# Twelve linear-attention layers and a feed-forward block: TensorE's steps of the middle layers in a written order

## The chip, the cores and the metric

The kernel runs on one core of a Trainium2 chip. The metric is the time of one execution on the device, in microseconds (us); lower is better. The engines are called PE (TensorE; PEld is its weight loads), DVE (VectorE), ACT (ScalarE), POOL (GpSimd) and SP (SyncE, which here only issues transfers).

## The reference

The input is 16 sequences of 256 tokens with 128 features. It passes 12 attention layers without softmax, a layer norm over input plus result, a feed-forward block with 384 hidden features and integer weights, and a second layer norm.

```python
for i in range(12):                      # 16 heads of 8 features
    q, k, v = split(x @ Wqkv[i].T + bqkv[i])
    att = einsum('bhqd,bhkd->bhqk', q, k) / sqrt(8)
    x = einsum('bhqk,bhkd->bhqd', att, v) @ Wproj[i].T + bproj[i] + x
x = layernorm(x0 + x)
h = silu(x @ (w_gate/127).T) * (x @ (w_up/127).T)
x = layernorm(x + h @ (w_down/127).T)
```

## The kernel before

Without a softmax a layer is linear in its tokens, so the kernel never carries the 256 tokens through the layers. For each sequence it carries a state of 128 x 130 numbers (`tst`): what the layers so far have made of a token's 128 features, and a column for the offsets (biases and means). The Gram matrix G of the centred tokens (`g0`) is computed once, in the prologue. One layer is then, for each pair of sequences (`thl` is the state as a rounded part hi and a residual lo, `whl` the weights in the same way):

1. k and v (`kv`): six matmuls of 256 columns of the state with the weights (lines 439 to 441), three for each sequence: hi with the rounded weights, hi with their residual, lo with the rounded weights. A copy brings them from the bank to `kv`.
2. G v (line 460): two full-precision matmuls of 128 columns, which the profile shows as four rows; a copy to `gv`.
3. q (lines 447 to 449): three matmuls of 260 columns; a copy, and a small DVE operation for the offsets (line 453).
4. M = k' G v, head group by head group (line 504): small matmuls of 32 x 32 tiles for all four pairs of a set at once. With it run the offset products (line 385), which multiply the offset column of a set's states with the weights. DVE makes of them `vb`, `kb`, a transpose and their product `kvo` (lines 395 to 400 and 212), adds `kvo` to M (line 514, `gm`) and multiplies with a mask (line 212).
5. y (line 522): 32 small matmuls, `gm` with q.
6. The projection (lines 539 to 541): y is copied to a rounded part and a residual (`yhl`, lines 204, 206 and 535), three matmuls follow for each pair, and DVE adds the result to the state (line 546). ACT rounds the state to hi (line 204, `thl`), POOL subtracts to lo (line 209). With these the next layer begins.

The 16 sequences form eight pairs, and these two sets of four; the sets run half a layer apart, so that PE works on one while the other engines work on the other. A half-layer on PE holds one run of M, one of y, 24 matmuls for k and v, 12 for q, 12 projections and 8 for G v.

The order of the instructions isn't written by hand. The program text declares operations with costs, the values that they read and write, the engines that can do them and a due time (`prio`); `Plan.run` goes through a model of the engines' time, always takes a ready operation that can start first (among equals the one with the earliest due time), gives it an engine and a PSUM bank (eight of them), and emits it. Each engine then works through its own list in that order; semaphores make it wait where a value isn't there yet. Copies from banks can go to ACT or DVE, subtractions to lo to POOL alone.

The due times are in the main loop: set `o` of layer `l` is due at `l + 0.5 * o`, q 0.3 later (`QLATE`), and the offsets' DVE work 0.3 later (`OFFSET`). From layer 2 on (`OWN`) the offset products of one set ride in the M run of the other: `heads(l, o, ...)` gets the rider `(l + o, 1 - o)`. In steady state the planner's order for PE is: offsets and M; one pair's q; k and v of two pairs of the other set; y; k and v of the other two; one G v; the projections; three G v; three pairs' q; and the same again for the other set.

Beside the layers, each layer's weights are loaded, rounded to `whl` (by DVE mostly, line 206), their residual subtracted (POOL, line 209), and turned copies of the projection weights made by transfers (`wpt`). In the last two layers and after them comes the feed-forward block for the eight pairs (`ffn`), with its norms on DVE (`st`), POOL and ACT.

Of the kernel before, what the change touches and what calls it, by code (L numbers as in the profile page):

```python
# [14 lines left out]
ALU = mybir.AluOpType  # L15
# [3 lines left out]
L = 12  # L19
# [21 lines left out]


OSTEP = 0.5
OFFSET = 0.3
LATE = 0.02
OWN = 2
DEEP = 0.5
QLATE = 0.3
FOFF = -1
FSTEP = 0.15  # L50
LSTEP = 0.05
# [41 lines left out]
class Plan:  # L93
# [23 lines left out]
    def run(self):  # L117
# [8 lines left out]
        while ready:  # L126
            found = []
            for o in ready:
                if any(not slots[v.kind] for v in takes(o)):
                    continue  # L130
                held = max((min(slots[v.kind])[0] for v in takes(o)), default=0.0)
                best, least = None, None
                for e, c in o.costs.items():
                    t = max(free[e], held)
                    for d in o.deps:
                        wait = TO_PE if e == PE and d.engine in (ACT, DVE, POOL) else 30 if d.engine == e == PE else AFTER[d.engine]
                        t = max(t, d.end + wait)
# [32 lines left out]
def mmr(n):  # L170
    return max(111, 0.447 * n + 5)
# [19 lines left out]
def linear_attention_ffn_kernel(ctx: ExitStack, tc: tile.TileContext, x, xt, wall, wq0, bias, wg, wu, wd, out):  # L191
# [228 lines left out]
    gms = [new(f"gm{o}", [OB, 32]) for o in range(NO)]  # L420
    vgm = sets()

    def products(l, p, prio):

        raw, whv, _ = wts[l]
        bs = slice(p * PB, (p + 1) * PB)
        hl = lambda i, s, n=1: whl[whv.slot][:, i, s * C : (s + n) * C]
        hi, lo = thl[p][:, 0], thl[p][:, 1]
        kv, qs, gv = kvs[p], qss[p], gvs[p]
        if l == 0:  # L430
            tv = lambda b: wraw[raw.slot][:, 2 * C : 3 * C]
            src = raw
        else:
            pkv, pq = Val("bank"), Val("bank")

            def mm_kv(e):
                for b in range(PB):
                    o = bank(pkv)[:, b * 2 * C : (b + 1) * 2 * C]
                    nc.tensor.matmul(o, hi[:, b, 0:C], hl(0, 1, 2), start=True, stop=False)  # L439
                    nc.tensor.matmul(o, hi[:, b, 0:C], hl(1, 1, 2), start=False, stop=False)  # L440
                    nc.tensor.matmul(o, lo[:, b, 0:C], hl(0, 1, 2), start=False, stop=True)  # L441
            plan.op({PE: 6 * mmr(256)}, mm_kv, [vhi[p], vlo[p], whv], [pkv], prio)
            plan.op({ACT: act(512), DVE: dve(512)}, lambda e: copy(e, kv.rearrange("p a b c -> p (a b c)"), bank(pkv)), [pkv], [vkv[p]], prio)

            def mm_q(e):
                o = bank(pq)[:, : PB * W]
                nc.tensor.matmul(o, hl(0, 0), flat(hi), start=True, stop=False)  # L447
                nc.tensor.matmul(o, hl(0, 0), flat(lo), start=False, stop=False)  # L448
                nc.tensor.matmul(o, hl(1, 0), flat(hi), start=False, stop=True)  # L449
            plan.op({PE: 3 * mmr(PB * W)}, mm_q, [vhi[p], vlo[p], whv], [pq], prio + QLATE)  # L450
            q = lambda: bank(pq)[:, : PB * W].rearrange("p (b w) -> p b w", w=W)
            plan.op({ACT: act(PB * C), DVE: dve(PB * C)}, lambda e: copy(e, qs[:, :, 0:C], q()[:, :, 0:C]), [pq], [vq[p]], prio + QLATE)
            plan.op({DVE: 130}, lambda e: nc.vector.tensor_scalar(qs[:, :, C], q()[:, :, C], bcol[:, l, 0:1], None, ALU.add), [pq, vbias], [vqo[p]], prio + QLATE)  # L453
            tv = lambda b: kv[:, b, 1, :]
            src = vkv[p]
        pgv = Val("bank")

        def mm_gv(e):
            for b in range(PB):
                nc.tensor.matmul(bank(pgv)[:, b * C : (b + 1) * C], g0[p][:, b, :], tv(b), start=True, stop=True)  # L460
        plan.op({PE: 2 * mm32()}, mm_gv, [vg0[p], src], [pgv], prio)
        plan.op({ACT: act(256), DVE: dve(256)}, lambda e: copy(e, flat(gv), bank(pgv)[:, : PB * C]), [pgv], [vgv[p]], prio)
        if l == L - 1:

            def rest(e):
                copy(e, tst[:, bs, 0:C], center.unsqueeze(1).to_broadcast([128, PB, C]))
                copy(e, tst[:, bs, C], mb[:, bs])
            plan.op({ACT: act(PB * C, True) + 100, DVE: dve(PB * C, True) + 75}, rest, [vhi[p], vlo[p], vmb], [vt[p], vc[p]], prio)

    def first_q(o, prio):  # L470

# [11 lines left out]
    def heads(l, o, prio, riders):  # L483

        raw = wts[l][0]
        pairs = range(o * G, (o + 1) * G)
        gm = gms[o]
        pm, pys = Val("bank"), [Val("bank") for _ in pairs]  # L490
        group = lambda g: slice(32 * (g % G), 32 * (g % G) + 32)
        src = [raw] if l == 0 else [vkv[p] for p in pairs]

        more = [(*r, *offset_products(*r)) for r in riders]

        def mm_m(e):
            for _, _, _, _, mm in more:
                mm()
            for p in pairs:
                for b in range(PB):  # L500
                    n = (p - o * G) * PB + b
                    tk = wraw[raw.slot][:, C : 2 * C] if l == 0 else kvs[p][:, b, 0, :]
                    for g in range(G):
                        nc.tensor.matmul(bank(pm)[group(g), n * 32 : n * 32 + 32], tk[:, group(g)], gvs[p][:, b, group(g)], start=True, stop=True)  # L504
        reads = [v for _, _, rs, _, _ in more for v in rs]
        if l == 0 and o == 1:

            reads += vw[:G]
        plan.op({PE: 890 + 140 * len(more)}, mm_m, [*(vgv[p] for p in pairs), *src, *reads], [pm, *(m[3] for m in more)], prio)
        for lo, oo, _, pc, _ in more:  # L510
            offsets(lo, oo, prio + (OFFSET if lo else 0), pc)
            if lo == 0:
                first_offsets(o, prio)
        plan.op({DVE: dve(OB * 32)}, lambda e: nc.vector.tensor_tensor(
            gm, bank(pm)[:, : OB * 32].rearrange("p (b j) -> p b j", j=32), kvo[:, o * OB : (o + 1) * OB], ALU.add), [pm, vkvo[o]], [vgm[o]], prio)
        plan.op({DVE: dve(OB * 32), POOL: pool(OB * 32)}, lambda e: mul(e, gm, gm, mask32.unsqueeze(1).to_broadcast([128, OB, 32])), [], [vgm[o]], prio)

        def mm_y(e):
            for b in range(PB):
                for r, p in enumerate(pairs):  # L520
                    for g in range(G):
                        nc.tensor.matmul(bank(pys[r])[group(g + r), b * W : (b + 1) * W], gm[group(g), r * PB + b, :], qss[p][group(g), b, :], start=True, stop=True)  # L522
        plan.op({PE: 1200}, mm_y, [vgm[o], *(vq[p] for p in pairs), *(vqo[p] for p in pairs)], pys, prio)
        return pys

    def projection(l, p, py, prio):
# [10 lines left out]
        def mm_w(e):  # L537
# [7 lines left out]
        plan.op({PE: (3 if l < L - 1 else 5) * mmr(PB * W)}, mm_w, [vyh[p], vyl[p], vhi[p], vlo[p], whv, turned], [pw, vw[p]], prio)  # L545
        plan.op({DVE: dve(PB * W)}, lambda e: nc.vector.tensor_tensor(ts, bank(pw)[:, : PB * W], ts, ALU.add), [pw], [vt[p], vc[p]], prio)  # L546
        if l < L - 1:
            plan.op({ACT: act(PB * W, True)}, lambda e: copy(e, flat(hi), ts), [vt[p], vc[p]], [vhi[p]], prio)
# [168 lines left out]
    for l in range(L):  # L717
        if l + 1 < L:
            prep_weights(l + 1)
        for o in range(NO):  # L720
            at = l + OSTEP * o
            for p in range(o * G, (o + 1) * G):
                products(l, p, at)
            for r, py in enumerate(heads(l, o, at, [(l, o)] * (l < OWN) + [(l + o, 1 - o)] * (OWN <= l + o < L))):
                projection(l, o * G + r, py, at + (LSTEP * r if l == L - 1 else 0))
        if l < NP:
            center_tokens(l, l + 2)
    prep_ffn(L - 2)
# [34 lines left out]
```

## Time and profile before

| | us |
|---|---|
| median of three runs | 309.67 (308.54 to 309.88) |
| the profiled execution | 309.26 |
| its span | 307.20 |
| PE busy (share of the span) | 297.3 (97%) |
| DVE busy | 227.2 (74%) |
| ACT busy | 221.3 (72%) |
| POOL busy | 136.4 (44%) |

The profile is of one execution. Its span runs from the first to the last instruction that it shows; about 2 us lie outside. Busy times are those in which an engine had an instruction in it; matmuls overlap in PE, so a full-width matmul of 256 columns shows a length of 0.28 us but the next one starts 0.12 us later, and starts are what to compare. The mean clock that the throttle granted PE over the span is 0.989 of full speed.

### The profile page before, as it was taken

What the parts mean: (1) busy time and instruction counts of PE and PEld (TensorE: products, weight loads), DVE (VectorE), ACT (ScalarE), POOL (GpSimd) and SP (SyncE); (2) the same over time, 40 slices, a digit from 0 to 9 for tenths busy, and PEclk for the clock granted to TensorE, in tenths of its full rate; (3) what the DMA queues carried; (4) which work ended last, traced back from release to release, by engine and by line L of the source; (5) the groups of instructions that cost most, each with busy time, mean ns of one, the idle gap of its engine ahead of it and who ended that gap; (6) DMA issues with size and microseconds to landing.
All of it is one profiled execution on the core that took longest, in us unless ns stands there. A gap on an engine that the chain in (4) does not pass through costs nothing.

```text
span 307.2 us, 12904 instructions
## 1 busy us (share of the span) xinstructions
PE 297.3 (97%) x5384; PEld 272.3 (89%) x5384; DVE 227.2 (74%) x680; ACT 221.3 (72%) x571; POOL 136.4 (44%) x234
## 2 busy tenths in 40 slices
PE   8999999999999999999999999999999999999971
PEld 8989999999999999999999999999999988888840
DVE  3797887777677676776767877787554699899993
ACT  2547877867768677777677666776986768968964
POOL 6246353334541345314453144521442456568582
PEclk9999999999999999999999999999999999999995
DMA  7534213122031120311202112130000000000214
GB/s 211 149 99 128 71 39 89 35 55 71 9 82 38 42 84 2 90 37 43 82 4 53 38 28 55 30 81 2 4 2 3 2 1 2 0 0 22 83 34 137
DMA packets 22489, 15.65 MB, mean 51 GB/s; under 512 B 1952, under 2 KB 19872, under 8 KB 22432
## 3 DMA queue, kind: packets, MB, share of 16 engines
q1 hardware_dynamic: 21872, 14.62, 17.5%
q8 instruction: 42, 0.69, 0.9%
q10 hardware_dynamic: 560, 0.22, 0.3%
q14 instruction: 15, 0.12, 0.1%
HBM read 8.02 MB, written 2.10 MB: 33 GB/s over the span
## 4 chain that ended last, share of the span: by engine, by line
PE 88%; DVE 7%; ACT 3%; issue 1%; POOLq 0%; POOL 0%
PE bank L460 14%; PE bank L439 8%; PE bank L522 8%; PE bank L441 7%; PE bank L440 7%; PE bank L447 5%; PE bank L504 5%; PE bank L541 4%; PE bank L539 4%; PE bank L540 4%; PE bank L448 3%; PE bank L449 3%; PE bank L341 3%; PE bank L665 2%; PE bank L681 2%; PE bank L682 2%
## 5 line engine op out<-in xcount | busy, mean ns | idle before, releaser
L209 POOL TENSOR_TENSOR thl<-tst,thl 128x260 fp32r<-128x260 f32 x88 | 64.5, 764 | 122.9 <-ACT thl L204 122.9
L204 ACT COPY qgv<-bank 128x256 f32<-128x256 f32 x171 | 60.8, 376 | 20.5 <-PE bank L449 13.5
L204 ACT COPY kv<-bank 128x512 f32<-128x512 f32 (+1 forms) x93 | 53.3, 575 | 18.6 <-PE bank L441 13.4
L439 PE MATMUL bank<-whl,thl 128*128 128x256 f32 x176 | 51.8, 294 | 0.0
L441 PE MATMUL bank<-whl,thl 128*128 128x256 f32 x176 | 49.6, 282 | 0.0
L440 PE MATMUL bank<-whl,thl 128*128 128x256 f32 x176 | 49.4, 281 | 0.0
L460 PE MATMUL bank<-kv,g 128*128 128x128 f32 x352 | 46.0, 275 | 0.0
L546 DVE TENSOR_TENSOR tst<-bank,tst 128x260 f32<-128x260 f32 x96 | 36.9, 425 | 11.9 <-PE bank L541 9.1
L204 ACT CAST thl<-tst 128x260 fp32r<-128x260 f32 x88 | 33.0, 408 | 14.6 <-DVE tst L546 14.5
L460 PEld LDWEIGHTS bank<-kv,g 128*128 128x128 f32 x352 | 42.7, 191 | 0.4 <-issue 0.4
L453 DVE TENSOR_SCALAR qgv<-bank,bcol 128x2 f32<-128x2 f32 x88 | 19.3, 221 | 27.6 <-ACT qgv L204 23.0
L439 PEld LDWEIGHTS bank<-whl,thl 128*128 128x128 f32 x176 | 33.1, 188 | 4.1 <-issue 4.0
L535 DVE TENSOR_TENSOR yhl<-bank,yhl 128x260 fp32r<-128x260 f32 x96 | 34.3, 421 | 2.4 <-ACT yhl L204 2.4
L440 PEld LDWEIGHTS bank<-whl,thl 128*128 128x128 f32 x176 | 33.2, 189 | 0.0
L441 PEld LDWEIGHTS bank<-whl,thl 128*128 128x128 f32 x176 | 33.1, 188 | 0.0
L447 PE MATMUL bank<-thl,whl 128*128 128x260 f32 x88 | 29.0, 329 | 0.0
L522 PE MATMUL bank<-qgv,gm 32*32 32x130 f32 x1536 | 25.9, 280 | 0.2 <-DVE gm L212 0.2
L204 ACT CAST yhl<-bank 128x260 fp32r<-128x260 f32 (+1 forms) x61 | 22.3, 418 | 5.2 <-PE bank L522 3.8
L206 DVE CAST yhl<-bank 128x260 fp32r<-128x260 f32 x43 | 16.5, 424 | 11.8 <-PE bank L522 11.8
L448 PE MATMUL bank<-thl,whl 128*128 128x260 f32 x88 | 24.8, 282 | 0.0
L449 PE MATMUL bank<-thl,whl 128*128 128x260 f32 x88 | 24.7, 281 | 0.0
L522 PEld LDWEIGHTS bank<-qgv,gm 32*32 32x32 f32 x1536 | 17.3, 103 | 5.6 <-ACT kv L204 0.3
(153 smaller groups left out, 705.8 us busy)
## 6 DMA issues: line engine op xcount, KB each, us to landing
wraw<-wall SPq DMA_DIRECT2D x12, 256.0 KB, 3.0
wpt<-whl SPq DMA_DIRECT2D x24, 96.0 KB, 2.2
qgv<-x SPq DMA_DIRECT2D x8, 256.0 KB, 5.4
xt<-xt SPq DMA_DIRECT2D x8, 256.0 KB, 3.3
out<-kv SPq DMA_DIRECT2D x7, 256.0 KB, 2.3
wpt<-whl SPq DMA_DIRECT2D x24, 64.0 KB, 2.6
wpt<-whl SPq DMA_DIRECT2D x24, 32.0 KB, 1.9
wraw<-wg SPq DMA_DIRECT2D x1, 192.0 KB, 3.4
```

The lines of the kernel that those rows point to most:

```text
L204: nc.scalar.copy(dst, src)
L209: (nc.vector if e == DVE else nc.gpsimd).tensor_tensor(dst, a, b, ALU.subtract)
L439: nc.tensor.matmul(o, hi[:, b, 0:C], hl(0, 1, 2), start=True, stop=False)
L440: nc.tensor.matmul(o, hi[:, b, 0:C], hl(1, 1, 2), start=False, stop=False)
L441: nc.tensor.matmul(o, lo[:, b, 0:C], hl(0, 1, 2), start=False, stop=True)
L447: nc.tensor.matmul(o, hl(0, 0), flat(hi), start=True, stop=False)
L448: nc.tensor.matmul(o, hl(0, 0), flat(lo), start=False, stop=False)
L449: nc.tensor.matmul(o, hl(1, 0), flat(hi), start=False, stop=True)
L460: nc.tensor.matmul(bank(pgv)[:, b * C : (b + 1) * C], g0[p][:, b, :], tv(b), start=True, stop=True)
L522: nc.tensor.matmul(bank(pys[r])[group(g + r), b * W : (b + 1) * W], gm[group(g), r * PB + b, :], qss[p][group(g), b, :], start=True, stop= ...
L535: plan.op({DVE: dve(PB * W)}, lambda e: nc.vector.tensor_tensor(yl, bank(py)[:, : PB * W], yh.bitcast(F32), ALU.subtract), [py, vyh[p]], [ ...
L546: plan.op({DVE: dve(PB * W)}, lambda e: nc.vector.tensor_tensor(ts, bank(pw)[:, : PB * W], ts, ALU.add), [pw], [vt[p], vc[p]], prio)
```

## The change

The one function that declared q, k, v and G v of a pair (`products`) is cut into `keys_values`, `queries` and `gram_values`; the M step (`heads`) and the y step (`outputs`) become two functions as well. In the layers from 1 to 10 each of PE's operations also writes a value `order` that stands for nothing but the order: as each must wait for the one declared before it, PE's list there is exactly that of the main loop. A run of M for set `o` of layer `l` is followed by k and v of the other set's next step (layer `l + o`, set `1 - o`), its G v, then y of set `o`, q of the other set, and the projections of set `o`. The matmuls for k and v are declared in two parts, two with hi alone and then the other four, but in the middle layers they stand side by side. The offset products of a set now run in the set's own M run, in all layers. The due times for q and for the offsets' DVE work lose their delay, and in the planner's model a PE operation that needs another PE operation no longer waits 30 ns for it. All engines but PE, and PE in layer 0 and in layer 11 with the feed-forward block, are still planned as before.

In the order of the built program the other engines differ as follows: 13 copies of G v move from DVE to ACT, and ten of the adds of the projection bias to the offset column (`share`, lines 405 and 407) from POOL to ACT. The number of matmuls of each kind is the same.

The main loop and the pieces that set the order:

```diff
-OFFSET = 0.3
-OWN = 2
-QLATE = 0.3
...
-                        wait = TO_PE if e == PE and d.engine in (ACT, DVE, POOL) else 30 if d.engine == e == PE else AFTER[d.engine]
+                        wait = TO_PE if e == PE and d.engine in (ACT, DVE, POOL) else 0 if d.engine == e == PE else AFTER[d.engine]
...
+    order = Val()
+    line = lambda l: [order] if 0 < l < L - 1 else []
+
+    def keys_values(l, p, prio):
...
+        def mm_hi(e, b=0):
+            o = bank(pkv)[:, b * 2 * C : (b + 1) * 2 * C]
+            nc.tensor.matmul(o, hi[:, b, 0:C], hl(0), start=True, stop=False)
+            nc.tensor.matmul(o, hi[:, b, 0:C], hl(1), start=False, stop=False)
+        plan.op({PE: 2 * mmr(256)}, mm_hi, [vhi[p], whv], [pkv, *line(l)], prio)
+
+        def mm_lo(e):
+            for b in range(PB):
+                if b:
+                    mm_hi(e, b)
+                nc.tensor.matmul(bank(pkv)[:, b * 2 * C : (b + 1) * 2 * C], lo[:, b, 0:C], hl(0), start=False, stop=True)
+        plan.op({PE: 4 * mmr(256)}, mm_lo, [vlo[p], whv], [pkv, *line(l)], prio)
...
-        plan.op({PE: 3 * mmr(PB * W)}, mm_q, [vhi[p], vlo[p], whv], [pq], prio + QLATE)
+        plan.op({PE: 3 * mmr(PB * W)}, mm_q, [vhi[p], vlo[p], whv], [pq, *line(l)], prio)
...
-        plan.op({PE: 2 * mm32()}, mm_gv, [vg0[p], src], [pgv], prio)
+        plan.op({PE: 2 * mm32()}, mm_gv, [vg0[p], *src], [pgv, *line(l)], prio)
...
-        more = [(*r, *offset_products(*r)) for r in riders]
+        offs, pc, mm_c = offset_products(l, o)
 
         def mm_m(e):
-            for _, _, _, _, mm in more:
-                mm()
+            mm_c()
             for p in pairs:
...
-        plan.op({PE: 890 + 140 * len(more)}, mm_m, [*(vgv[p] for p in pairs), *src, *reads], [pm, *(m[3] for m in more)], prio)
-        for lo, oo, _, pc, _ in more:
-            offsets(lo, oo, prio + (OFFSET if lo else 0), pc)
-            if lo == 0:
-                first_offsets(o, prio)
+        plan.op({PE: 1030}, mm_m, [*(vgv[p] for p in pairs), *src, *reads], [pm, pc, *line(l)], prio)
+        offsets(l, o, prio, pc)
+        if l == 0:
+            first_offsets(o, prio)
...
-        plan.op({PE: 1200}, mm_y, [vgm[o], *(vq[p] for p in pairs), *(vqo[p] for p in pairs)], pys, prio)
+        plan.op({PE: 1200}, mm_y, [vgm[o], *(vq[p] for p in pairs), *(vqo[p] for p in pairs)], [*pys, *line(l)], prio)
...
         for o in range(NO):
-            at = l + OSTEP * o
-            for p in range(o * G, (o + 1) * G):
-                products(l, p, at)
-            for r, py in enumerate(heads(l, o, at, [(l, o)] * (l < OWN) + [(l + o, 1 - o)] * (OWN <= l + o < L))):
-                projection(l, o * G + r, py, at + (LSTEP * r if l == L - 1 else 0))
+            at, pairs = l + OSTEP * o, range(o * G, (o + 1) * G)
+            if l == 0:
+                for p in pairs:
+                    gram_values(l, p, at)
+            heads(l, o, at)
+            if l == L - 1:
+                for p in pairs:
+                    rest(p, at)
+
+            ln, on = l + o, 1 - o
+            then = range(on * G, (on + 1) * G) if 0 < ln < L else []
+            for f in (keys_values, gram_values):
+                for p in then:
+                    f(ln, p, ln + OSTEP * on)
+            pys = outputs(l, o, at)
+            for p in then:
+                queries(ln, p, ln + OSTEP * on)
+            for r, p in enumerate(pairs):
+                projection(l, p, pys[r], at + (LSTEP * r if l == L - 1 else 0))
```

`rest`, which fills the states anew for the last layer's result, is the old code of `products` under a name of its own.

More of the change, by code (lines that the diff above doesn't have):

```diff
@@ L421, in linear_attention_ffn_kernel @@
     vgm = sets()
-    def products(l, p, prio):
-        raw, whv, _ = wts[l]
+    order = Val()
+    line = lambda l: [order] if 0 < l < L - 1 else []
+    def keys_values(l, p, prio):
+        _, whv, _ = wts[l]
+        hl = lambda i: whl[whv.slot][:, i, C : 3 * C]
+        hi, lo, kv = thl[p][:, 0], thl[p][:, 1], kvs[p]
+        pkv = Val("bank")
+        def mm_hi(e, b=0):
[9 more added lines that the diff above has]
+        plan.op({PE: 4 * mmr(256)}, mm_lo, [vlo[p], whv], [pkv, *line(l)], prio)
+        plan.op({ACT: act(512), DVE: dve(512)}, lambda e: copy(e, kv.rearrange("p a b c -> p (a b c)"), bank(pkv)), [pkv], [vkv[p]], prio)
@@ new lines, in queries, with mm_q @@
+    def queries(l, p, prio):
+        _, whv, _ = wts[l]
+        hl = lambda i: whl[whv.slot][:, i, 0:C]
+        hi, lo, qs = thl[p][:, 0], thl[p][:, 1], qss[p]
+        pq = Val("bank")
+        def mm_q(e):
+            o = bank(pq)[:, : PB * W]
+            nc.tensor.matmul(o, hl(0), flat(hi), start=True, stop=False)
+            nc.tensor.matmul(o, hl(0), flat(lo), start=False, stop=False)
+            nc.tensor.matmul(o, hl(1), flat(hi), start=False, stop=True)
+        plan.op({PE: 3 * mmr(PB * W)}, mm_q, [vhi[p], vlo[p], whv], [pq, *line(l)], prio)
+        q = lambda: bank(pq)[:, : PB * W].rearrange("p (b w) -> p b w", w=W)
+        plan.op({ACT: act(PB * C), DVE: dve(PB * C)}, lambda e: copy(e, qs[:, :, 0:C], q()[:, :, 0:C]), [pq], [vq[p]], prio)
+        plan.op({DVE: 130}, lambda e: nc.vector.tensor_scalar(qs[:, :, C], q()[:, :, C], bcol[:, l, 0:1], None, ALU.add), [pq, vbias], [vqo[p]], prio)
@@ L426, in products, with gram_values @@
+    def gram_values(l, p, prio):
+        raw = wts[l][0]
         bs = slice(p * PB, (p + 1) * PB)
-        hl = lambda i, s, n=1: whl[whv.slot][:, i, s * C : (s + n) * C]
-        hi, lo = thl[p][:, 0], thl[p][:, 1]
-        kv, qs, gv = kvs[p], qss[p], gvs[p]
+        gv = gvs[p]
         if l == 0:
             tv = lambda b: wraw[raw.slot][:, 2 * C : 3 * C]
-            src = raw
+            src = [raw]
         else:
[L434 to L449, printed above, removed]
-            plan.op({PE: 3 * mmr(PB * W)}, mm_q, [vhi[p], vlo[p], whv], [pq], prio + QLATE)
[L451 to L455, printed above, removed]
@@ L456, in products @@
+            tv = lambda b: kvs[p][:, b, 1, :]
+            src = [vkv[p]]
         pgv = Val("bank")
@@ L460, in mm_gv, with rest, fill @@
                 nc.tensor.matmul(bank(pgv)[:, b * C : (b + 1) * C], g0[p][:, b, :], tv(b), start=True, stop=True)
-        plan.op({PE: 2 * mm32()}, mm_gv, [vg0[p], src], [pgv], prio)
+        plan.op({PE: 2 * mm32()}, mm_gv, [vg0[p], *src], [pgv, *line(l)], prio)
         plan.op({ACT: act(256), DVE: dve(256)}, lambda e: copy(e, flat(gv), bank(pgv)[:, : PB * C]), [pgv], [vgv[p]], prio)
[L463 to L468, printed above, removed]
+    def rest(p, prio):
+        bs = slice(p * PB, (p + 1) * PB)
+        def fill(e):
+            copy(e, tst[:, bs, 0:C], center.unsqueeze(1).to_broadcast([128, PB, C]))
+            copy(e, tst[:, bs, C], mb[:, bs])
+        plan.op({ACT: act(PB * C, True) + 100, DVE: dve(PB * C, True) + 75}, fill, [vhi[p], vlo[p], vmb], [vt[p], vc[p]], prio)
     def first_q(o, prio):
@@ L481, in first_offsets, with heads @@
         plan.op({POOL: 600}, fill, [vqc[o]], vqo[o * G : (o + 1) * G], prio)
-    def heads(l, o, prio, riders):
+    group = lambda g: slice(32 * (g % G), 32 * (g % G) + 32)
+    def heads(l, o, prio):
         raw = wts[l][0]
@@ L489, in heads @@
         gm = gms[o]
-        pm, pys = Val("bank"), [Val("bank") for _ in pairs]
-        group = lambda g: slice(32 * (g % G), 32 * (g % G) + 32)
+        pm = Val("bank")
         src = [raw] if l == 0 else [vkv[p] for p in pairs]
-        more = [(*r, *offset_products(*r)) for r in riders]
+        offs, pc, mm_c = offset_products(l, o)
         def mm_m(e):
-            for _, _, _, _, mm in more:
-                mm()
+            mm_c()
             for p in pairs:
@@ L504, in mm_m @@
                         nc.tensor.matmul(bank(pm)[group(g), n * 32 : n * 32 + 32], tk[:, group(g)], gvs[p][:, b, group(g)], start=True, stop=True)
-        reads = [v for _, _, rs, _, _ in more for v in rs]
+        reads = offs
         if l == 0 and o == 1:
             reads += vw[:G]
-        plan.op({PE: 890 + 140 * len(more)}, mm_m, [*(vgv[p] for p in pairs), *src, *reads], [pm, *(m[3] for m in more)], prio)
-        for lo, oo, _, pc, _ in more:
-            offsets(lo, oo, prio + (OFFSET if lo else 0), pc)
-            if lo == 0:
-                first_offsets(o, prio)
+        plan.op({PE: 1030}, mm_m, [*(vgv[p] for p in pairs), *src, *reads], [pm, pc, *line(l)], prio)
+        offsets(l, o, prio, pc)
+        if l == 0:
+            first_offsets(o, prio)
         plan.op({DVE: dve(OB * 32)}, lambda e: nc.vector.tensor_tensor(
@@ L516, in heads, with outputs @@
         plan.op({DVE: dve(OB * 32), POOL: pool(OB * 32)}, lambda e: mul(e, gm, gm, mask32.unsqueeze(1).to_broadcast([128, OB, 32])), [], [vgm[o]], prio)
+    def outputs(l, o, prio):
+        pairs, gm = range(o * G, (o + 1) * G), gms[o]
+        pys = [Val("bank") for _ in pairs]
         def mm_y(e):
@@ L544, in mm_w @@
                 nc.tensor.matmul(o, centerr, flat(lo), start=False, stop=True)
-        plan.op({PE: (3 if l < L - 1 else 5) * mmr(PB * W)}, mm_w, [vyh[p], vyl[p], vhi[p], vlo[p], whv, turned], [pw, vw[p]], prio)
+        plan.op({PE: (3 if l < L - 1 else 5) * mmr(PB * W)}, mm_w, [vyh[p], vyl[p], vhi[p], vlo[p], whv, turned], [pw, vw[p], *line(l)], prio)
         plan.op({DVE: dve(PB * W)}, lambda e: nc.vector.tensor_tensor(ts, bank(pw)[:, : PB * W], ts, ALU.add), [pw], [vt[p], vc[p]], prio)
```

## The prediction

> **What bounds the kernel now.** I read the page's first two parts, then the list of TensorE's (PE's) waits, then the windows, and last the timeline of two seams between steps.
>
> The page's parts 1 and 2 (busy time; busy tenths in 40 slices):
>
> ```profile
> PE 297.3 (97%) x5384; PEld 272.3 (89%) x5384; DVE 227.2 (74%) x680; ACT 221.3 (72%) x571; POOL 136.4 (44%) x234
> PE   8999999999999999999999999999999999999971
> ```
>
> PE is full from the second slice to the last but two. All that PE waited for, and three windows (us, then busy time of PE, PEld, DVE, ACT and POOL):
>
> ```profile
> PE bank L702 <- DVE xt L696: 2.0, 2, 1.2
> PE bank L224 <- DVE qgv L222: 1.0, 1, 1.0
> PE bank L694 <- DVE hl L209: 0.6, 1, 0.6
> PE bank L541 <- DVE yhl L535: 0.2, 1, 0.2
> PE bank L522 <- DVE gm L212: 0.2, 1, 0.2
> ```
>
> ```profile
> 100.00:140.00 40.00, 40.00 (x883) 37.43 (x884) 28.70 (x88) 29.69 (x78) 15.96 (x22) 1.00 0.18 49
> 290.00:300.00 10.00, 7.58 (x36) 5.24 (x34) 9.28 (x24) 6.90 (x17) 9.10 (x11) 1.00 0.19 52
> 300.00:307.20 7.20, 1.12 (x4) 0.71 (x4) 2.01 (x7) 2.80 (x8) 1.40 (x3) 0.51 0.53 146
> ```
>
> In the layers there are two waits of 0.2 us, both in layer 0. From 100 to 140 us PE has no gap at a granted clock of 1.00. The other two waits (2.0 and 0.6 us) belong to the feed-forward end after 290 us. So the layers can become faster only if PE's own instructions take less, and any new wait of PE in them is paid in full.
>
> **What the new order does to PE's own time.** The built program has the same 3391 matmuls, kind by kind; 19 times in a row it runs offsets and M, 24 matmuls for k and v, 8 for G v, y, 12 for q, 12 projections. What an order can save is what PE loses between kinds. Timeline of PE (start, length):
>
> ```profile
> 119.94 0.28 PE L449 MATMUL bank<-thl,whl 128*128 128x260 f32 x1
> 120.15 0.31 PE L385 MATMUL bank<-tst,wraw 128*32 128x8 f32 x16
> 120.30 0.76 PE L504 MATMUL bank<-qgv,kv 128*32 128x32 f32 x64
> 120.98 0.39 PE L447 MATMUL bank<-thl,whl 128*128 128x260 f32 x1
> 121.20 0.28 PE L448 MATMUL bank<-thl,whl 128*128 128x260 f32 x1
> ...
> 122.75 0.28 PE L441 MATMUL bank<-whl,thl 128*128 128x256 f32 x1
> 122.95 1.07 PE L522 MATMUL bank<-qgv,gm 32*32 32x130 f32 x64
> 123.96 0.38 PE L439 MATMUL bank<-whl,thl 128*128 128x256 f32 x1
> ```
>
> From one full-width matmul to the next it is 0.12 us; into a run of small tiles 0.20 to 0.21 (119.94 to 120.15, 122.75 to 122.95), and after it 0.22 for the first step. So M and y cost about 0.1 at each end, four times a half-layer. The new order has the same four ends: projection to offsets, M to k and v, G v to y, y to q. [...]
>
> ```profile
> 46.38 0.61 PE L460 MATMUL bank<-kv,g 128*128 128x128 f32 x4
> 46.91 1.07 PE L522 MATMUL bank<-qgv,gm 32*32 32x130 f32 x64
> ```
>
> 0.53 us for four rows: three steps of 0.112 (1.34 us for 12 rows in the chain of waits) and 0.20. No discount. New half-layer: offsets 0.15 + M 0.68 + k and v 0.22 + 23 x 0.1187 = 2.95 + G v 15 x 0.112 + 0.20 = 1.88 + y 1.01 + q 0.22 + 11 x 0.1205 = 1.55 + projections 11 x 0.1205 + 0.21 = 1.54: 9.76 us. Now the offsets start at 81.26, 90.99 and 100.74 in the chain, 9.74 apart. The sum is no finer than 0.02; I take 0, and -0.2 to +0.4 us over 19 half-layers.
>
> **What comes closer on the other engines.** Today one run of G v and most of q lie between the projections and the next k and v. Afterwards only the offsets and M do. The path is: projection, DVE adds it to the state, ACT rounds it (hi), POOL subtracts (lo), PE multiplies lo for k and v. Its pace now (timelines of PE, DVE, ACT, POOL):
>
> ```profile
> 116.42 0.28 PE L541 MATMUL bank<-yhl,whl 128*128 128x260 f32 x1
> 116.81 1.52 DVE L546 TENSOR_TENSOR tst<-bank,tst 128x260 f32<-128x260 f32 x4 [0.58 <-PE bank L541]
> 117.32 1.11 ACT L204 CAST thl<-tst 128x260 fp32r<-128x260 f32 x3 [0.54 <-DVE tst L546]
> 117.81 2.85 POOL L209 TENSOR_TENSOR thl<-tst,thl 128x260 fp32r<-128x260 f32 x4 [6.32 <-ACT thl L204]
> ```
>
> Count from S, the first pair's last projection matmul (116.42). The first lo starts at S + 1.36 (1.39 here; 1.34 at 126.18 to 127.52), four take 2.85: done at S + 4.21. PE: the last projection starts at S + 1.08, offsets S + 1.29, M, k and v at S + 2.12; the fourth pair's first lo product is the 21st matmul: 2.12 + 0.22 + 19 x 0.1187 = S + 4.60. Its weights go in 0.12 earlier, and 0.05 passes between POOL's end and PE (in the seam below lo ends at 25.38, the weights start at 25.43): lo has to be done by S + 4.43. Margin 0.22.
>
> But POOL does not keep 2.85. In every other half-layer, with DVE's weight cast in it, the four take 3.03:
>
> ```profile
> 108.04 3.03 POOL L209 TENSOR_TENSOR thl<-tst,thl 128x260 fp32r<-128x260 f32 x4 [5.61 <-ACT thl L204]
> ```
>
> ```profile
> 108.15 0.91 DVE L206 CAST whl<-wraw 128x512 fp32r<-128x512 f32 x1
> ```
>
> The cast waited for POOL and one lo came out at 0.92 instead of 0.74. The new order also brings DVE's kvo product into this stretch (four adds to S + 1.81, four q offsets of 0.135 each, vb, kb, transpose, then kvo at about S + 3.1); now it runs while POOL idles (0.42 us at 123.10). In the seam of layer 0, which already has the new shape, kvo costs one lo just the same (0.937), and there PE's matmul at 25.43 came 0.1 us late. So one blocked lo per half-layer: S + 1.36 + 3.04 = S + 4.40 against 4.43. I take 0.03 us of stall per seam, 19 seams, 0.6 us; the ends are 0 and, with cast and kvo both blocking, 0.16 x 19 = 3.0.
>
> [...] The rows above show a loss of 0.18 to 0.19, and the sum goes by them.
>
> **Other moves, costed at nothing, with their cover.** (1) The offsets' bank is the second projection's: its add ends at S + 0.39 + 0.36 + 0.42 = 1.17, PE wants it at 1.29; cover 0.1. [...] (3) After y the first residual yl is ready 2.1 us from y's start (124.64 + 0.42 against 122.95), the first projection comes at 1.01 + 1.55 = 2.56. (4) The k, v copies on ACT (0.59, ready each 0.71) end at S + 5.9, the last G v starts at 6.4. (5) The share adds, ten more on ACT (0.31) and off POOL, fall between the last hi (S + 2.3) and the first k, v copy (S + 3.2); the 13 copies of G v that leave DVE (0.42) cost ACT 0.37 each ahead of y's copies. SP's transfers keep their order; its weights still come a layer ahead.
>
> **The two ends.** In layer 1 two G v matmuls now precede y, which covers the 0.2 us wait for gm: -0.2. In layer 11 and the first feed-forward steps the programs differ, then from the first down-projection on PE's orders agree, and DVE's nearly so. PE has no gap there now (220 to 270 us), so what can come is loss: 0 to 1 us; I take 0.2.
>
> **Sum.** The profiled execution took 309.26 us, of which the span is 307.20. 309.26 + 0 + 0.6 - 0.2 + 0.2 = 309.86; the median of the runs is 0.41 above this execution, so 310.2. About 0.5% (1.55 us) can be told from no change: below 308.1 is faster, above 311.2 slower.
>
> **Rivals.** (a) Slower: POOL's lo chain becomes the bound of each seam. For it: a margin of 0.03 and the late matmul at 25.43. It decides once two of four subtractions are blocked, or the chain starts 0.1 later: 0.1 to 0.35 us per seam, 19 seams, 2 to 6.6 us, 312 to 317. Against: kvo finds the last lo already running in the half-layers with the cast. (b) Faster: VectorE enters the feed-forward end with less behind it, and the 2.0 + 0.6 us that PE waits there go: 307.6. Against: until 274 us the chain runs over PE, and the order after that is the same. (c) That the order isn't what it says: excluded, the built program shows it 19 times.
>
> **Chances.** Small stalls 0.57, (a) 0.30, (b) 0.13. The range reaches into (a) to 313.4 and into (b) to 307.9.
>
> **What would show it.** Right: the offsets stay 9.74 to 9.85 apart in the chain, POOL's four lo read 3.0, PE's list of waits shows a few tenths at the lo products. (a): those waits add up to microseconds, with DVE's gm product or POOL named. Wrong altogether: a half-layer below 9.70, which would mean that the ends of the small-tile runs cost less in the new order, or over 10.2, a wait that I did not see, at y or the projections.

## The result, and the profile after

The changed kernel takes 310.69 us (median of ten runs, 310.31 to 312.1) against 309.55 us for the kernel before (median of ten, 308.54 to 310.66) on the same chip. The ratio is 1.0045, with a 95% interval of 1.0026 to 1.0064: a little slower, by 0.8 to 2.0 us. The profiled execution took 310.84 us, its span 307.8.

The page's first two parts after (busy time and instructions; busy tenths of PE in 40 slices), and the list of what PE waited for (total, times, longest, in us):

```profile
PE 297.3 (97%) x5384; PEld 272.1 (88%) x5384; DVE 229.8 (75%) x665; ACT 232.1 (75%) x598; POOL 136.6 (44%) x222
PE   8989999999999999999999999999999999999971
```

```profile
PE bank L725 <- DVE xt L719: 2.0, 2, 1.2
PE bank L221 <- DVE qgv L219: 1.0, 1, 1.0
PE bank L564 <- DVE yhl L558: 0.8, 1, 0.8
PE bank L717 <- DVE hl L206: 0.6, 1, 0.6
```

PE's busy time is the same to a tenth of a microsecond (297.3), and the 2.0 and 0.6 us of the feed-forward end are there as before. One wait is gone (gm, 0.2 us), one has grown from 0.2 to 0.8 us: the first projection's residual, in layer 0. The window from 100 to 140 us (its length, then busy time of PE, PEld, DVE, ACT and POOL, the clock, and the transfers) still shows no gap of PE at a clock of 1.00:

```profile
100.00:140.00 40.00, 40.00 (x842) 37.62 (x841) 30.14 (x87) 31.76 (x81) 14.93 (x18) 1.00 0.19 49
```

By these views nothing has happened in the layers. That is misleading. A full-width matmul shows a length of 0.28 us and the next one normally starts after 0.12, so a lateness of up to 0.16 us leaves no gap at all. The loss has to be read from starts. I took the start of every run of offset products (line 385 before, 382 after) and the start of the first down-projection (the product that opens it) from the trace. Between them lie four stretches. Differences of starts are the same whatever the prologue's transfers do (the first offsets start anywhere between 13.7 and 14.9 us in the executions below), and whatever the tail does (from the last down-projection to the end 12.4 to 13.1 us).

| stretch, us | before | after | difference |
|---|---|---|---|
| layer 0: first offsets to second | 7.74 | 8.41 | +0.67 |
| second to fifth | 29.70 | 30.35 | +0.65 |
| fifth to twenty-second, 17 half-layers | 165.41 | 166.04 | +0.63 |
| twenty-second to first down-projection | 44.67 | 44.28 | -0.39 |
| sum | 247.52 | 249.08 | +1.56 |

From the first down-projection to the last it is 32.02 us in both. So the end is shifted, not changed, and three losses of nearly equal size want an explanation.

**The middle layers.** Twelve half-layers in the steady part take 9.740 us each before (71.44 to 188.32) and 9.771 after (72.59 to 189.84): 0.031 more. Here is the seam that begins at S = 110.41 us, the first pair's last projection matmul (timeline of POOL, DVE and PE; start, length):

```profile
111.80 3.05 POOL L206 TENSOR_TENSOR thl<-tst,thl 128x260 fp32r<-128x260 f32 x4 [5.23 <-ACT thl L201]
112.72 0.82 DVE L203 CAST whl<-wraw 128x512 fp32r<-128x512 f32 x1
...
114.03 0.28 PE L433 MATMUL bank<-whl,thl 128*128 128x256 f32 x1
114.15 0.28 PE L434 MATMUL bank<-whl,thl 128*128 128x256 f32 x1
114.19 0.94 DVE L209 TENSOR_TENSOR kvo<-vbb,kb 128x256 f32<-128x256 f32 x1
114.26 0.32 PE L441 MATMUL bank<-whl,thl 128*128 128x256 f32 x1
114.42 0.28 PE L433 MATMUL bank<-whl,thl 128*128 128x256 f32 x1
```

The first lo starts at S + 1.39 and the four are done at S + 4.44. The lo product of line 441, the third pair's first, has the next matmul only 0.16 us after it, where 0.12 is usual; its pair's lo ended 0.05 us before its weights went in. The 24 matmuls for k and v take 2.954 us in this seam, from first start to the next step's, and 2.972 to 2.976 us in the other steady ones, where the lateness is spread over several steps. Half of these seams have a weight cast on DVE, as here; there the weights of the third and of the fourth pair's lo product go in 0.05 us behind POOL's end. In the other half it is 0.07 us for the fourth pair and 0.2 for the rest.

**Layer 0.** Timeline of POOL, DVE and PE; brackets give the idle time ahead of a row and what ended it:

```profile
18.70 1.27 POOL L206 TENSOR_TENSOR whl<-wraw,whl 128x512 fp32r<-128x512 f32 x1 [1.72 <-ACT whl L201]
18.85 1.40 DVE L203 CAST whl<-wraw 128x512 fp32r<-128x512 f32 x1
20.17 0.75 DVE L203 CAST yhl<-bank 128x260 fp32r<-128x260 f32 x2
...
21.31 0.39 PE L564 MATMUL bank<-yhl,whl 128*128 128x260 f32 x1 [0.83 <-DVE yhl L558]
```

y starts at 18.49 us. DVE's rounding of a layer's weights, 0.42 us in the kernel before, comes 0.15 us behind POOL's subtraction of another layer's residual and takes 1.40. The roundings of y queue behind it.

**The seam at 43 us.** Timeline of the same engines and ACT:

```profile
38.77 0.91 ACT L366 ACTIVATE xt<-xt,nmeans 128x256 f32<-128x256 f32 x2
39.58 0.64 ACT L201 CAST yhl<-bank 128x260 fp32r<-128x260 f32 x2
41.98 1.43 DVE L569 TENSOR_TENSOR tst<-bank,tst 128x260 f32<-128x260 f32 x4
43.05 3.42 POOL L206 TENSOR_TENSOR thl<-tst,thl 128x260 fp32r<-128x260 f32 x4 [8.04 <-ACT thl L201]
44.44 0.43 DVE L209 TENSOR_TENSOR kvo<-vbb,kb 128x256 f32<-128x256 f32 x1
45.25 0.28 PE L434 MATMUL bank<-whl,thl 128*128 128x256 f32 x1
45.43 0.42 DVE L209 TENSOR_TENSOR gm<-gm,mask 128x256 f32<-128x256 f32 x1
45.53 0.39 PE L441 MATMUL bank<-whl,thl 128*128 128x256 f32 x1
```

ACT centres tokens (`xt`) just ahead of y's roundings, the residuals and adds on DVE are late, and POOL's four lo take 3.42 us, with kvo and the mask product inside them. PE's k and v take 3.49 us.

### The profile page after: what moved, and what is told of

Its sections match the earlier page's. It is cut to its first block, busy times and chain, and to the rows that moved or that the text cites. A ratio compares the mean times of both kernels' runs of the same rounds, so it can differ in the third digit from the quotient of the medians.

```text
span 307.8 us, 13115 instructions
## 1 busy us (share of the span) xinstructions
PE 297.3 (97%) x5384; PEld 272.1 (88%) x5384; DVE 229.8 (75%) x665; ACT 232.1 (75%) x598; POOL 136.6 (44%) x222
## 4 chain that ended last, share of the span: by engine, by line
PE 91%; DVE 6%; ACT 1%; issue 1%; POOLq 0%; POOL 0%; DVEq 0%
PE bank L477 13%; PE bank L433 8%; PE bank L545 8%; PE bank L441 7%; PE bank L434 7%; PE bank L454 5%; PE bank L522 5%; PE bank L564 4%; PE bank L562 4%; PE bank L563 4%; PE bank L455 3%; PE bank L456 3%; PE bank L704 3%; PE bank L705 3%; PE bank L338 3%; PE bank L688 2%
## 5 line engine op out<-in xcount | busy, mean ns | idle before, releaser
L206 POOL TENSOR_TENSOR thl<-tst,thl 128x260 fp32r<-128x260 f32 x88 | 67.3, 796 | 128.7 <-ACT thl L201 128.7
L201 ACT COPY qgv<-bank 128x256 f32<-128x256 f32 x184 | 67.8, 377 | 9.6 <-PE bank L477 2.6
L203 DVE CAST yhl<-bank 128x260 fp32r<-128x260 f32 (+1 forms) x44 | 17.3, 430 | 36.3 <-PE bank L545 36.3
L477 PE MATMUL bank<-kv,g 128*128 128x128 f32 x352 | 43.5, 275 | 0.0
L201 ACT CAST thl<-tst 128x260 fp32r<-128x260 f32 x88 | 31.4, 408 | 14.0 <-DVE tst L569 13.9
L477 PEld LDWEIGHTS bank<-kv,g 128*128 128x128 f32 x352 | 41.4, 192 | 0.4 <-issue 0.4
L569 DVE TENSOR_TENSOR tst<-bank,tst 128x260 f32<-128x260 f32 x96 | 36.2, 427 | 3.1 <-PE bank L567 1.2
L201 ACT CAST yhl<-bank 128x260 fp32r<-128x260 f32 (+1 forms) x60 | 21.6, 413 | 8.0 <-PE bank L545 6.3
L454 PE MATMUL bank<-thl,whl 128*128 128x260 f32 x88 | 27.3, 311 | 0.0
L455 PE MATMUL bank<-thl,whl 128*128 128x260 f32 x88 | 24.8, 282 | 0.0
L456 PE MATMUL bank<-thl,whl 128*128 128x260 f32 x88 | 24.8, 282 | 0.0
L632 POOL TENSOR_TENSOR rs<-ve,mhalf 128x4 f32<-128x4 f32 x16 | 17.4, 1090 | 11.0 <-DVE ve L626 7.5
```

Of the source, the lines that this page charges most:

```text
L201: nc.scalar.copy(dst, src)
L206: (nc.vector if e == DVE else nc.gpsimd).tensor_tensor(dst, a, b, ALU.subtract)
L454: nc.tensor.matmul(o, hl(0), flat(hi), start=True, stop=False)
L455: nc.tensor.matmul(o, hl(0), flat(lo), start=False, stop=False)
L456: nc.tensor.matmul(o, hl(1), flat(hi), start=False, stop=True)
```

## The experiments

My theory: PE's own time doesn't depend on which of the two orders it has; the losses are the lo chain's margin (0.03 us a seam), one order on DVE in layer 0 and one late seam. The rival throughout: PE itself is slower in the written order, or the offsets' new place is to blame. All ratios are against the kernel before, run on the same chip.

**One part alone: the offsets in their own M run.** The kernel before, with one number changed.

```diff
-OWN = 2
+OWN = L
```

> The kernel before with one part of the change alone: offset products in their own set's M run in all layers, the tensor engine still ordered by the planner. Theory (the loss of the changed kernel is the thin margin of the lo chain, about 0.03 us a seam, and one late seam in the early layers): without the new order one G v and most of q still stand between the projections and k, v, so a lo that kvo blocks is covered; no change, 309.2 to 309.9 us, offsets 9.74 us apart. Rival 1 (the offsets' DVE work in the new place is itself the loss): 310.4 to 311. Rival 2 (the loss is in PE's own time in the written order): no change either, as with the theory.

309.43 us, ratio 1.0025 (1.001 to 1.004). This edit reaches layer 11 too, where the kernel before overwrites the offset column ahead of M, so its offset products there work on other numbers and what it computes is not the block. The middle doesn't lose: from the second offsets to the twenty-second it is 194.91 us against 195.11. The loss of 1.08 us lies behind the twenty-second. So I ran it again, with layer 11 as before.

```diff
-OWN = 2
+OWN = L - 1
```

> The kernel before with the offset products in their own set's M run in layers 0 to 10, and layer 11 as before. With layer 11 changed too, the stretch from the offsets of layer 0's second set to the twenty-second offsets took as long as before, and all of the extra 1 us came behind it. Theory (the offsets' place costs nothing as long as q and a G v stand between the projections and k, v): total 0.999 to 1.001 of the kernel before, k, v matmuls 2.945 us for 24. Rival (the DVE work of the offsets in the new place delays the copies that PE waits for): 1.002 or more.

308.46 us, ratio 0.9988 (0.9971 to 1.0006), and 247.22 us from the first offsets to the first down-projection. The offsets' place costs nothing while q and a G v stand between the projections and k, v. It was layer 11 that cost 1 us in the run before.

**More cover for the lo chain.** The changed kernel, with the fourth pair's q behind the projections.

```diff
-            for p in then:
+            for p in then[:3]:
                 queries(ln, p, ln + OSTEP * on)
             for r, p in enumerate(pairs):
                 projection(...)
+            for p in then[3:]:
+                queries(ln, p, ln + OSTEP * on)
```

> The changed kernel with the fourth pair's q behind the projections. That puts three matmuls (0.36 us) more between the projections and k, v, and brings the first projection 0.36 us nearer to y (its residual is ready 2.1 us from y's start, its product would come at about 2.4). Theory: the 24 k, v matmuls fall from 2.97 to 2.94 us, the half-layer from 9.765 to 9.735 us, and the late seam at 43 us loses most of its 0.55 us: about 0.5 to 1 us less than the changed kernel, 309.7 to 310.2 us. Rival (PE's own time is longer in the written order, whatever the lo chain does): half-layer still 9.765 us, 310.4 to 311 us. If the margin at the projections were the thin one instead, a loss: over 311 us with waits for yl.

The 24 matmuls fall to 2.952 to 2.958 us and twelve half-layers take 9.743 us each (72.46 to 189.38): 0.028 of the 0.031 is back, 0.019 of it at k and v, the rest at q and the projections, whose order the edit changes. The stretch of 17 half-layers falls by 0.39 us. In the seam at 43 us they fall to 3.00 us, but layer 1's lo products are now later (24 matmuls in 3.46 us, 3.21 in the changed kernel), so the second stretch gains only 0.10. The total, 310.32 us, ratio 1.0043 (1.0022 to 1.0064), misses the forecast, but it is too coarse for half a microsecond; the profiled execution also drew a tail 0.66 us longer than the changed kernel's.

**Less: the lo chain slowed.** The changed kernel, each subtraction cut in two.

```diff
-lambda e: sub(e, flat(lo), ts, flat(hi).bitcast(F32))
+lambda e: [sub(e, lo[:, b], tst[:, p * PB + b], hi[:, b].bitcast(F32)) for b in range(PB)]
```

> The changed kernel with each pair's subtraction to lo as two POOL instructions of half the columns. The weights' residual (512 columns, 1.27 us) against a lo (260 columns, 0.71 us) gives about 0.13 us fixed per instruction, so four pairs' lo end about 0.5 us later. Theory (no margin is left at the fourth lo): each of 19 seams becomes about 0.5 us longer, half-layer about 10.25 us, 318 to 322 us in all, with PE's waits at the lo products. Rival (the chain has slack of some tenths and the 0.03 us are PE's own): at most 0.2 us a seam, 311 to 314.5 us.

319.97 us, ratio 1.0371 (1.0342 to 1.04). Twelve half-layers take 10.296 us each (74.52 to 198.07), 0.525 more. Timeline of POOL and PE at one seam:

```profile
115.76 4.04 POOL L206 TENSOR_TENSOR thl<-tst,thl 128x130 fp32r<-128x130 f32 x8 [5.09 <-ACT thl L201]
118.50 0.28 PE L434 MATMUL bank<-whl,thl 128*128 128x256 f32 x1
118.83 0.39 PE L441 MATMUL bank<-whl,thl 128*128 128x256 f32 x1
```

POOL's four pairs take 3.87 to 4.04 us in place of 3.04, 0.83 to 1.0 more. Of this, 0.44 to 0.62 us arrives at k and v (3.42 and 3.60 us in place of 2.976 and 2.972); the row at 118.83, a lo product, starts 0.33 us after the matmul ahead of it. The other 0.38 us is nearly what the cut itself allows: the chain now ends with half a pair, which only the 24th matmul needs, where a whole pair was needed by the 21st, 0.36 us earlier. So there is no slack of several tenths: the chain's end and PE's need lie within hundredths of each other. That the half-layer grew by the forecast 0.5 us is partly luck, as the chain grew by nearly twice the forecast. And PE's list of waits for this kernel has the same four lines as above and no other, although PE lost 9.4 us between the two marks.

**PE's own time: two runs of small tiles side by side.** The written order changed so that offsets and M of one set follow y of the other, with one pair's q ahead of the projections and three behind.

```diff
-            heads(l, o, at)
             ...
             pys = outputs(l, o, at)
-            for p in then:
+            if then:
+                heads(ln, on, nxt)
+            for p in then[:1]:
                 queries(ln, p, nxt)
             ...
+            for p in then[1:]:
+                queries(ln, p, nxt)
```

> The written order with y of one set and then offsets and M of the other set side by side, so that two runs of small tiles stand next to each other: k and v, G v, y of the other set, offsets and M, one pair's q, the projections, three pairs' q. The q behind the projections keep the lo chain covered by about 0.3 us more than in the changed kernel. Theory (PE's own time depends on its order only by what it loses at each end of a run of small tiles, about 0.1 us): two of four ends go, 0.2 us from each of 19 half-layers, 9.53 to 9.56 us each, 305.5 to 307 us in all. Rival (changing from y's 32x32 tiles to the 128x32 tiles of the offsets costs as much as an end, or something else hides behind what is called an end): half-layer 9.7 us or more, 309 to 311 us.

310.5 us, ratio 1.0054 (1.0031 to 1.0077). Half of the theory holds: the steps at their undelayed lengths add up to 9.53 us (q 0.46, projections 1.44, q 1.09, k and v 2.83, G v 1.88, y 1.00, offsets 0.15, M 0.685), so the 0.2 us are there. But M itself is held up in 11 of the 17 half-layers of the middle stretch, by 0.07 to 0.71 us, 2.9 in all, and in some of the others k and v take 2.94. The stretch is 166.08 us long, as in the changed kernel, and the total is the rival's. Timeline of PE, then its list of waits:

```profile
126.81 0.31 PE L382 MATMUL bank<-tst,wraw 128*32 128x8 f32 x16
126.95 0.24 PE L522 MATMUL bank<-qgv,kv 128*32 128x32 f32 x6
127.38 0.72 PE L522 MATMUL bank<-qgv,kv 128*32 128x32 f32 x58 [0.18 <-issue]
```

```profile
PE bank L522 <- issue: 1.1, 4, 0.5
```

"issue" means that PE waited for nothing that the profile shows; the copies of G v that M reads were done at 126.34. What stands out is the number of instructions: y, offsets and M are 144 matmuls and 144 weight loads in 1.84 us. The trace has a queue of instruction packets, 42 in number (0.69 MB, so 16 KB each), each 0.9 to 1.5 us long:

```profile
q8 instruction: 42, 0.69, 0.9%
```

They keep step with PE: in the changed kernel 10506 matmuls and weight loads start between the first packet's start and the 42nd's, on the mean 256 from one packet to the next. Count PE's recorded instructions (matmuls, weight loads, the sequencer's) in order of start: eight of the eleven hold-ups, 2.6 of the 2.9 us, end at instruction 193 or 194 past a multiple of 256, and 1.37 to 1.46 us after one of these packets ended. The four longest:

| from the matmul ahead to the next start, us | next start | instruction, past a multiple of 256 | last packet ended | next start minus packet's end, us |
|---|---|---|---|---|
| 0.40 | 68.86 | 194 | 67.42 | 1.44 |
| 0.38 | 127.38 | 194 | 125.92 | 1.46 |
| 0.44 | 167.03 | 194 | 165.62 | 1.41 |
| 0.71 | 196.64 | 193 | 195.26 | 1.38 |

In the changed kernel's 17 middle half-layers PE passes that place (instruction 193) 2.1 us or more after a packet, and no M is held up. One M here passed it 1.24 us after a packet and wasn't held up either, so the delay isn't fixed. That M waits there for instructions that such a packet brings is the author's estimate from these times; no run varied it. The other three hold-ups (0.07 to 0.12 us) stand elsewhere and stay open.

**Layer 0.** The changed kernel, with the weights of layers 1 and 2 rounded on ACT alone.

```diff
+        on = {ACT: act(n, True)} if 1 <= l <= 2 else {ACT: act(n, True), DVE: dve(n, True)}
-        plan.op({ACT: act(n, True), DVE: dve(n, True)}, lambda e: copy(e, whl[...], wraw[...]), ...)
+        plan.op(on, lambda e: copy(e, whl[...], wraw[...]), ...)
```

> The changed kernel with the rounding of the weights of layers 1 and 2 on ACT alone. In the changed kernel DVE's second rounding of 512 columns takes 1.40 us in place of 0.42, because POOL's subtraction of the weights' residual (1.27 us) began 0.15 us before it, and the copies of layer 0's first y stand behind it: PE's first projection waits 0.83 us. Theory (this one order is layer 0's whole loss): from the offsets of set 0 to those of set 1 in layer 0, 8.40 us now, becomes 7.7 to 7.8 us as in the kernel before, and the total falls by 0.6 to 0.7 us, 1.002 to 1.003 of the kernel before. Rival (the wait comes from y's products or the casts on ACT): still 8.3 to 8.4 us there, total as the changed kernel's, 1.0045.

Layer 0 takes 7.74 us, exactly as before the change, and the total is 309.77 us, ratio 1.0007 (0.9991 to 1.0024), a little under the forecast: between the two marks it is 0.96 us less, as the second stretch (0.10) and the middle (0.18) gain too. The timeline (ACT, DVE, PE) shows the rounding on ACT and the first product with y's residual 0.33 us behind the matmul ahead of it in place of 1.11:

```profile
18.41 0.62 ACT L201 CAST whl<-wraw 128x512 fp32r<-128x512 f32 x1
19.04 0.76 DVE L203 CAST yhl<-bank 128x260 fp32r<-128x260 f32 x2 [0.55 <-PE bank L546]
20.20 0.39 PE L565 MATMUL bank<-yhl,whl 128*128 128x260 f32 x1
```

**The seam at 43 us.** The changed kernel, with the centring of tokens held back.

```diff
-..., [vn], [vx[p]], prio)
+..., [vn, vhi[NP - 1]], [vx[p]], prio)
```

> The changed kernel with the centring of the tokens (two ACT instructions of 0.45 us per layer, layers 0 to 7) held back until the layer's last hi cast, so that it doesn't stand ahead of the casts of y. In the changed kernel the seam at 41 to 46 us, where two of them run at 38.8 to 39.7 us just ahead of those casts, has late projections (1.66 in place of 1.53 us), late adds, and 24 k, v matmuls of 3.49 in place of 2.97 us. Theory (this seam is late because of that order): the three half-layers from 22.7 to 53.05 us, 30.35 us now, take 29.7 to 29.9; total about 0.5 us under the changed kernel. Rival (it is late because kvo and the mask product of DVE each block a lo there, whoever comes ahead): k, v still over 3.3 us at that seam, 30.2 us or more.

309.42 us, ratio 1.0015 (0.9999 to 1.003). The second stretch takes 29.69 us, 0.66 less; k and v take 2.98 there and POOL's four lo 3.04:

```profile
40.07 0.65 ACT L201 CAST yhl<-bank 128x260 fp32r<-128x260 f32 x2 [0.43 <-PE bank L545]
43.36 3.04 POOL L206 TENSOR_TENSOR thl<-tst,thl 128x260 fp32r<-128x260 f32 x4 [7.72 <-ACT thl L201]
```

The order on ACT was what made this seam late. The later stretches give 0.44 us of it back: two runs of projections take 1.6 and 1.8 us in place of 1.53.

**kvo without its second SBUF operand.** The changed kernel, with kb left in its bank.

```diff
-tensor_scalar(kb[:, bs], src(1), ...)
+tensor_scalar(src(1), src(1), ...)
...
-mul(e, kvo[:, bs], vbb[:, bs], kb[:, bs].unsqueeze(2)...)
+mul(e, kvo[:, bs], vbb[:, bs], src(1).unsqueeze(2)...)
```

> The changed kernel with DVE's kb left in its bank, so that the product kvo reads one operand from PSUM and one from SBUF in place of two from SBUF. Theory (the late lo of each second seam is DVE's kvo, with two SBUF operands, against POOL): kvo takes 0.42 to 0.45 us there in place of 0.94, POOL's four lo 2.85 in place of 3.05 us in the half-layers without a weight cast, and their 24 k, v matmuls 2.95 in place of 2.975 us; half-layer 9.755 on the mean, total 0.2 to 0.4 us under the changed kernel. Rival (any DVE instruction beside POOL costs the same): four lo still 3.03 to 3.05 us, half-layer 9.77.

kvo, minimum, median and maximum in ns, in the changed kernel and here:

```profile
L209 DVE TENSOR_TENSOR kvo<-vbb,kb x24: 416/770/941, 16.5 to 239.1; 128x256 f32<-128x256 f32 x24
```

```profile
L209 DVE TENSOR_TENSOR kvo<-vbb,bank x24: 407/420/423, 16.0 to 238.8; 128x256 f32<-128x256 f32 x24
```

It never waits now. In the half-layers without a weight cast the four lo take 2.86 us, in the others 3.05:

```profile
101.18 2.86 POOL L206 TENSOR_TENSOR thl<-tst,thl 128x260 fp32r<-128x260 f32 x4 [6.69 <-ACT thl L201]
110.94 3.05 POOL L206 TENSOR_TENSOR thl<-tst,thl 128x260 fp32r<-128x260 f32 x4 [5.43 <-ACT thl L201]
```

Eight half-layers from 62.05 to 140.11 us take 9.758 each, the theory's number, but not for its reason. Without a weight cast the fourth lo is done 0.17 us earlier, and the 24 matmuls for k and v still take 2.969 to 2.977 us (2.976 in the changed kernel). With a cast, where the lo end as before to within 0.01 us, the 24 take 2.952 to 2.959 in place of 2.972. So the lo that kvo blocks isn't what costs the 0.02 us where the theory had it, and what the gain is stays open. The total doesn't show it: 310.36 us, ratio 1.0036 (1.0021 to 1.0051). Layer 0 takes 8.86 us here, one run of projections 1.80, and the stretch ahead of the first down-projection is 0.87 us longer: the planner made other choices on DVE and ACT.

**The repairs together.** First all four, then without kb in its bank and with the centring held back for three pairs only.

> The changed kernel with four repairs together: the fourth pair's q behind the projections, kb in its bank, the weights of layers 1 and 2 rounded on ACT, the tokens centred after the last hi cast. Theory (the loss of 1.56 us from the first offsets to the first down-projection is layer 0's cast 0.66, one late seam 0.65, and 0.03 us for each of 17 to 19 seams, less 0.4 us gained at the beginning of the feed-forward block): 247.3 to 247.9 us there against 247.5 before and 249.1 in the changed kernel, and a total of 0.998 to 1.001 of the kernel before, no more. Rival (PE itself is slower in the written order): a total of 1.003 or more.

310.12 us, ratio 1.0029 (1.0014 to 1.0045), 249.34 us between the two marks: a miss. k and v are at 2.96 throughout, but six runs of y take 1.14 to 1.16 us in place of 1.004, again with nothing in the profile that they wait for, and layer 0 takes 8.16. These six stand at y's last two matmuls, at changing places in the count of 256 and 2.6 us or more after a packet, so they are not the hold-ups of M above; their cause is open. The total is at the edge of the rival's 1.003, and no run tells these hold-ups apart from PE's own time.

> The changed kernel with three repairs: the fourth pair's q behind the projections, the weights of layers 1 and 2 rounded on ACT, and the centring of the first three pairs' tokens held back until the layer's last hi cast. Theory (the losses of layer 0, of the seam at 43 us and of the thin margin add up): from the first offsets to the first down-projection 249.08 - 0.67 - 0.66 - 0.39 = 247.4 us against 247.5 before, total 0.999 to 1.001 of the kernel before; where PE has no wait left, the written order is worth nothing against the planner's. Rival (the order itself costs PE time, or the repairs only move the waits): 248.3 us or more, total 1.002 or more.

309.2 us, ratio 1.0001 (0.9981 to 1.0021). The total is the theory's, the stretches are not: 248.27 us, 0.9 more than the sum of the repairs and at the edge of the rival's 248.3: the repairs in part only move the waits. Layer 0 (7.73) and the second stretch (29.80) are repaired, but layer 1's k and v take 3.47 us, and in the middle two runs of projections take 1.68 us in place of 1.44 and one of k and v 3.15. With the q behind the projections the margin is thin there.

So none of these versions is measurably faster than the kernel before; the nearest, the offsets alone up to layer 10, has an interval that includes no change. The changed kernel with three repairs is level with it.

## Why the prediction was right, and where it was not

**PE's own time, taken as 0: right to about 0.02 us a half-layer.** The prediction's sum came to 9.76 us against 9.74 and was set to no difference, as too fine; the changed kernel takes 9.771, and 9.743 with the fourth pair's q moved. The terms came as summed: M 0.684, G v 1.878, y 1.004, and k and v 2.952 with more cover. The price of an end, 0.1 us, is confirmed from the other side: where two ends were taken away, the undelayed steps add up to 0.2 us less.

**The lo chain, 0.03 us a seam: its timing was right, that it makes the whole 0.03 isn't shown.** Forecast: done at S + 4.40 against a need at S + 4.43; measured S + 4.44, and 0.031 us a half-layer. That no margin is left is shown: a slower chain is paid at once. But only 0.02 of the 0.031 lies at k and v, where the chain would act. More cover takes that away; ending the fourth lo 0.17 us earlier does not. So the step that put the stall on one blocked lo per half-layer, through the fourth pair's product, isn't confirmed, and the cause of the 0.02 is open. The 0.63 us over the 17 half-layers meets the forecast of 0.6 partly by luck: the twelve steady ones give 0.37, and the first of the 17 alone gives 0.40, as it was short before (9.38 us, 9.77 after); a later one gives 0.16 back. A lo loses 0.19 us beside kvo (0.93 in place of 0.74), and a half-layer no more than 0.03. In layer 0 the loss is larger: POOL's subtraction had 1.12 us to run when the DVE cast began, and the cast took 0.98 us longer (1.40 in place of 0.42).

**Layer 1, taken as -0.2: the wait for gm did go, but the stretch lost 0.65.** The failing step is the one that set one blocked lo for every seam. In the seam at 43 us the chain also started late, and two DVE products fell into it. That is rival (a)'s mechanism and, at 0.5 us, more than its price of 0.1 to 0.35, in one seam instead of nineteen. What pushed it there stood on ACT, where I had counted only what the change moves in the steady layers.

**Layer 0, not in the sum at all: +0.67.** The list of "other moves, costed at nothing" is the step that failed: it went through the written order's half-layers and left out the layer that the planner still orders itself. There the kernel before had its 0.2 us wait on the same residual, so there was no margin for a rounding that moves ahead of it.

**The beginning of the feed-forward block, taken as +0.2: -0.39.** No experiment was made on it; it stays open.

**The sum.** Forecast +0.6 us, measured +1.56 between the two marks and +1.14 between the medians. The prediction of 310.2 was 0.5 low: two one-time losses, 1.32 us together, were not seen, and the gain of 0.39 at the feed-forward block wasn't either.

**What would show it: wrong view.** I expected a few tenths in PE's list of waits. It has none, and none even where 9.4 us were lost. The other two signs came: offsets 9.77 us apart, POOL's four lo at 3.05. **Rival (b)** is out: the 2.0 and 0.6 us stayed in every kernel here.

## What to carry to other kernels

Where the bounding engine has no gaps, count first what lies between kinds of instructions: here M (0.684 us) and y (1.004) took as long in both orders, and an end of such a run cost 0.1. Then look for the chain on the other engines whose cover the new order removes. Fixing one engine's order by hand makes a greedy planner choose differently for all the others, so the layers that the edit doesn't touch, the first above all, have to be checked as well. For effects of tenths of a microsecond compare starts of the same step between two marks, not waits or spans: the overlapped matmuls here (0.28 us long, 0.12 apart) hide a lateness of 0.16 us each. And where a sum agrees with the forecast, look whether it was gained in the places where the forecast had it.

## What was unexpected

Two runs of small tiles side by side, 288 instructions in 1.84 us, are held up by 0.07 to 0.71 us in 11 of 17 half-layers with no wait on another engine in the profile, 2.6 of 2.9 us of it at instruction 193 or 194 past a multiple of 256. In the kernels before and after, where the runs stand apart, M takes 0.684 us each time in the middle; y alone was held up by 0.12 to 0.16 us in a few places of two experiments. So most of the 0.2 us that merging saves on PE is lost again.

Not only DVE's product with two SBUF operands took longer beside POOL (kvo 0.94 us in place of 0.42): a cast with a single one, begun 0.15 us after POOL's subtraction, took 1.40 us, and 0.42 in the kernel before, where it began ahead of it (at 19.45 us, POOL at 19.53). The product with one operand in PSUM took 0.41 to 0.42 us in all 24 places.
